# Self-attention scores of a perceiver layer: by key alone, with the row of maxima spread through HBM and the values one token tile later

## The chip, the core and the metric

The kernel runs on one core of a Trainium2 chip, as one launch. The metric is the device time of that launch in microseconds (us), as the median of several runs. The engines of the core have their own instruction queues: TensorE (PE; its weight loads are shown apart as PEld), VectorE (DVE), ScalarE (ACT), GpSimd (POOL) and SyncE (SP), which issues most DMAs here. TensorE writes to PSUM, which this kernel uses as eight banks of 128 x 512 fp32; ScalarE and VectorE bring results from there to SBUF.

## The reference, cut to what matters

The input is x of 16 batches x 64 tokens x 1024, and a context of 16 x 1024 x 1024. Three blocks follow each other, each added to x:

```python
x = x + xattn(layernorm(x), ctx, ctx)    # 32 heads, 8 key/value heads, head size 32, 1024 keys a batch
x = x + attn(layernorm(x))               # the same heads, biases, rotary, 64 keys a batch
x = x + ffn(layernorm(x))                # ternary weights, 4-bit and 8-bit activations, 1024 -> 2752 -> 1024
```

The change is in the second block. What it computes there, per batch and head (four query heads share a key/value head):

```python
scores = einsum('bqhd,bkhd->bhqk', q, k) / sqrt(32)
probs  = softmax(scores, axis=-1)        # over the 64 keys of the batch
out    = einsum('bhqk,bkhd->bqhd', probs, v)
```

The softmax takes a maximum over the keys for each query and head, subtracts it, and divides by the sum of the exponentials.

## The kernel before

The 1024 tokens are 8 tiles of 128 tokens, so a tile holds two whole batches. The order of the work on every engine is the order in which the program names it: there is no planner. Side work for TensorE waits in a list, `fillers`, and each `fill(n)` in the program takes the next n of them. The loop over the tiles (L1242 to L1289) is the place of the change.

SBUF is one large tile, `arena`, in which buffers are placed by hand (`place`, in KB), and rings hand out two or more places in turn. PSUM has two banks `m0`, `m1` that `m_tile` gives in turn, two more (`t0`, `t1`) for transposes, and four for `w`, the scores and outputs of the attention. There is only one `w`.

**A tile of self attention** (class `Tile2`) needs the scores twice, since the maximum over the keys lies along the free dimension only when queries are the partitions, and the values need the keys as partitions:

- `by_query`: 32 matmuls give scores with queries as partitions in `w` (L770, K = 32 rows, four row groups of the array side by side); one VectorE reduction takes the maxima over 64 keys (L778).
- `shift` (`in_parts`, L539 to L546): four small VectorE instructions split each maximum into three bfloat16 parts.
- `turn`: eight TensorE transposes (L787) bring the parts under each other, one ScalarE copy (L793) takes them to SBUF.
- `by_key`: eight matmuls against a matrix of minus ones (L802, shown as L801) write the negative maxima into `w`, 16 fp32 matmuls (L813) add the scores with keys as partitions; ScalarE takes the exponential straight from PSUM (L821).
- `values`: 16 matmuls for the outputs (L834) and 16 for the sums (L845), both into `w`, three ScalarE copies (L853, L856).
- `finish`: 12 transposes into `w` (L866, L869), VectorE's reciprocal and two products (L871, L876), and POOL adds the result to the residual `xs[t]` (L882).

An fp32 matmul is shown as two instructions.

**Beside it.** With a tile's result in `xs[t]`, `quantize(t)` makes the 4-bit activations in three pieces: statistics (L179 to L185, with a power on POOL), normalize and the mean magnitude (L171, L914), and rounding (L917 to L925); `transpose3` turns them for the feed-forward part (L932, copied by ScalarE, L933).

**The fillers.** In the early tiles 0 to 3 they are 24 steps of `project2(1)`, the projections for batches 8 to 15: four halves for the two key chunks, four steps for v and 16 halves for the eight query chunks, where a half is the matmuls of four of the eight slices of the sum (L242) and a v step is a whole chunk (L730). A q or k chunk is taken from its bank by ScalarE with the bias (L709); then the rotary follows on VectorE (L710, L711) and POOL (L712, L713). A v chunk is taken by VectorE (L737). In the late tiles 4 to 7 the fillers are 32 calls of `gate_up` for the first four token tiles: eight matmuls for the gate into one bank, eight for the up part into the other (L950), a relu on ScalarE (L958), a product on VectorE (L959) and one on POOL (L962). A relu and a product per filler set the two `m` banks free. Two of the 24 run ahead of the loop and 6, 6, 5 and 5 in tiles 0 to 3. Ahead of tile 4 two gate/up steps run, then up to eight in each tile.

Behind the loop comes the rest of the feed-forward part: quantize of tile 7, and gate/up steps for tiles 4 to 7.

**The first attention** (class `Unit`) already works by key alone: VectorE collects maxima, turns them by 32x32 block transposes and reductions (L591 to L598), SP writes the row to HBM and reads it back to all partitions (L604, L605), VectorE subtracts it (L610) and ScalarE takes the exponential (L611).

Of the kernel before, what the change touches and what calls it, by code (L numbers as in the profile page):

```python
# [20 lines left out]
P = 128  # L21
# [28 lines left out]
def kernel(  # L50
# [33 lines left out]
    def t_tile(shape, dtype, name, n=None):  # L84

        turns["t"] ^= 1
        n = turns["t"] if n is None else n
        return ps_t.tile(shape, dtype, tag=f"t{n}", name=name)
# [14 lines left out]
    def place(kb, shape, dtype=F32):  # L103

        first, n = round(kb * 256), math.prod(shape) * mybir.dt.size(dtype)
        a = arena[:, first : first + (n + 3) // 4]
        if dtype != F32:
            a = a.bitcast(dtype)
        a = a[:, : math.prod(shape)]
        if len(shape) > 1:  # L110
            names = [f"a{i}" for i in range(len(shape))]
            sizes = dict(zip(names[1:], shape[1:]))
            a = a.rearrange(f"p ({' '.join(names)}) -> p {' '.join(names)}", **sizes)
        return a
# [46 lines left out]

    spilled = [dram.tile([P, DIM], F32, name=f"spilled{t}") for t in range(NT)]
    results = [dram.tile([P, DIM], F32, name=f"results{t}") for t in range(NT - 2)]
    tops = [dram.tile([1, 1024], F32, name=f"tops{i}") for i in range(2)]

    def layernorm(dst, src, name):
# [372 lines left out]
    def in_parts(to, m):  # L539

        rest = small.tile([P, 32], F32, tag="rest")
        rest = rest[:, : math.prod(m.shape[1:])].rearrange("p (a b) -> p a b", b=m.shape[2])
        nc.vector.tensor_copy(to[:, :, :, 0], m)
        nc.vector.tensor_tensor(rest, m, to[:, :, :, 0], ALU.subtract)
        nc.vector.tensor_copy(to[:, :, :, 1], rest)
        nc.vector.tensor_tensor(to[:, :, :, 2], rest, to[:, :, :, 1], ALU.subtract)  # L546
# [129 lines left out]
    n2s = {}  # L676
    kT2 = place(112, [2, B, NQ])
    v2 = place(120, [NT, KVD])
    sh2_ring = Ring(152, 154)
    oS = place(156, [2, 4, 2, NQ])  # L680
    sS = place(160, [4, 2, NQ])
    parts2 = [place(162 + 2 * i, [8, 4, HD], BF) for i in range(2)]
    p2_ring = Ring(136, 144)
    biased_ring = Ring(172, 174)
    turned_ring = Ring(168, 170)
# [70 lines left out]
    class Tile2:  # L756
# [3 lines left out]
        def __init__(self, t, w):  # L760
            self.t, self.w = t, w

        def by_query(self):
            t = self.t
            s = self.w.rearrange("p j (c k) -> p j c k", k=NQ)
            for c in range(8):
                b2, g, rp = c // 4, c // 2 % 2, c % 2
                for jj in range(4):
                    rows = bass.ts(jj, HD)
                    nc.tensor.matmul(  # L770
                        s[:, jj, c, :],
                        lhsT=qa[g][rows, bass.ds((2 * t + b2) * 256 + rp * P, P)],
                        rhs=kT2[rows, g, 2 * t + b2, :],
                        start=True,
                        stop=True,
                    )
            top = small.tile([P, 4, 8], F32, tag="top32", name=f"top2_{t}")
            nc.vector.tensor_reduce(top, s, AX.X, ALU.max)  # L778
            self.top = top

        def shift(self):
            in_parts(parts2[self.t % 2], self.top.rearrange("p j c -> p c j"))

        def turn(self):
            tp = t_tile([P, 8 * P], BF, f"shp2_{self.t}")
            for c in range(8):
                nc.tensor.transpose(  # L787
                    tp[:, bass.ts(c, P)],
                    parts2[self.t % 2][:, c].rearrange("p j k -> p (j k)"),
                    ident_b,  # L790
                )
            self.sh = sh2_ring.next([2, 2, 256], BF)
            nc.scalar.copy(self.sh.rearrange("p b g c -> p (b g c)"), tp)  # L793

        def by_key(self):
            t = self.t
            s = self.w.rearrange("p j (g c) -> p j g c", g=2)
            for b2 in range(2):
                for jj in range(4):
                    rows = bass.ts(jj, HD)  # L800
                    nc.tensor.matmul(  # L801
                        self.w[bass.ts(b2, NQ), jj, :],  # L802
                        lhsT=minus[rows, 0:NQ],
                        rhs=self.sh[rows, b2].rearrange("p g c -> p (g c)"),
                        start=True,
                        stop=False,
                    )
            for g in range(2):
                for b2 in range(2):
                    for jj in range(4):  # L810
                        rows = bass.ts(jj, HD)
                        b = 2 * t + b2
                        nc.tensor.matmul(  # L813
                            s[bass.ts(b2, NQ), jj, g, :],
                            lhsT=kT2[rows, g, b, :],
                            rhs=qa[g][rows, bass.ts(b, 256)],
                            start=False,
                            stop=(g == 1),
                        )
            self.p = p2_ring.next([4, 2, 256])  # L820
            nc.scalar.activation(  # L821
                self.p.rearrange("p j g c -> p (j g c)"),
                self.w.rearrange("p j c -> p (j c)"),
                AF.Exp,
                scale=SCALE,
            )

        def values(self):
            t, p, w = self.t, self.p, self.w
# [75 lines left out]
    def quantize(t):  # L905

        xn = place(xn3_at, [DIM])
        statistics, normalize = layernorm(xn, xs[t], f"n3_{t}")
        b = beta[:, t : t + 1]
        rb = small.tile([P, 1], F32, tag="rb", name=f"rb_{t}")  # L910

        def magnitude():
            normalize()
            nc.vector.tensor_reduce(b, xn, AX.X, ALU.add, apply_absolute_value=True)  # L914

        def rounded():
            nc.vector.tensor_scalar_mul(b, b, 1.0 / DIM)  # L917
            nc.vector.tensor_scalar_add(rb, b, EPS)
            nc.vector.reciprocal(rb, rb)
            nc.vector.tensor_scalar(xn, xn, SQRT7, rb, ALU.mult, ALU.mult)  # L920
            nc.vector.tensor_scalar(xn, xn, -8.0, 7.0, ALU.max, ALU.min)
            xq3[t] = place(xq_at, [DIM], BF)
            nc.vector.tensor_scalar(xq3[t], xn, MAGIC, MAGIC, ALU.add, ALU.subtract)
            nc.gpsimd.tensor_tensor(cgate[:, t : t + 1], b, wscale[:, 0:1], ALU.mult)
            nc.gpsimd.tensor_tensor(cup[:, t : t + 1], b, wscale[:, 1:2], ALU.mult)  # L925

        return [statistics, magnitude, rounded]
# [113 lines left out]
    def fill(n=1):  # L1041
        for _ in range(n):
            if fillers:
                fillers.pop(0)()

    with tc.manual_schedule():
# [174 lines left out]
        nc.sync.dma_start(bv_sb, bv.to_broadcast([P, KVD]))  # L1221
        for g in range(2):
            wqs2.append(load_queries(stream.next([4, KC, P]), wq2[g], nc.sync, 1))
        for p in parts2:
            nc.gpsimd.memset(p, 0.0)


        for n, step in enumerate(project2(0)):
# [10 lines left out]
        ps_w2 = ps_w_closed.enter_context(tc.tile_pool(name="ps_w2", bufs=1, space=PSUM))  # L1239
        w = ps_w2.tile([P, 4, 512], F32, name="w2")  # L1240
        fill(2)
        for t in range(NT):  # L1242
            two = Tile2(t, w)
            late = t >= NT // 2
            if t == NT // 2 - 2:
                for n in range(2):
                    fetch(n)
            if t == NT // 2:
                fill(len(fillers))
                fetch(2)  # L1250
                steps = [(n, tt) for n in range(NCH) for tt in range(NT // 2)]

                steps[:12] = [s for s in steps[:12] if s[1] < 3] + [(n, 3) for n in range(3)]

                def beside(n, tt):
                    gate_up(n, tt, lambda i: m_tile(f"gu_{n}_{tt}_{i}"))
                    if tt == NT // 2 - 1:
                        fetch(n + 3)

                fillers += [lambda s=s: beside(*s) for s in steps]  # L1260
                fill(2)
            pieces = quantize(t - 1) if t else []

            def piece():
                if pieces:
                    pieces.pop(0)()

            two.by_query()
            fill()
            two.shift()  # L1270
            fill()
            two.turn()
            fill()
            piece()
            if late:
                fill()
            piece()
            two.by_key()
            fill()
            piece()  # L1280
            if late:
                fill()
            two.values()
            fill()
            two.finish()
            if t:
                transpose3(t - 1)
            if t % 4 < 2 or late:
                fill()  # L1289
        fill(len(fillers))  # L1290

# [107 lines left out]
```

## Time and profile before

| | |
|---|---|
| median of 3 runs | 1881.87 us (1881.67 to 1883.24) |
| the profiled execution | 1883.46 us, span 1881.5 us |
| granted TensorE clock, mean | 0.997 |
| first and last scores by query of the self attention (L770) begin | 1488.6 and 1685.4 us |
| mean of one block transpose of 128x1024 (L591) | 1245 ns |
| mean of one subtraction of 128x2048 (L610) | 2957 ns |
| spread of a row to 128 partitions, 512 KB (L605), median landing | 4.4 us |

The page gives busy time and share of each engine, and groups of instructions by line. TensorE's weight loads overlap its matmuls, and a busy TensorE is not one at its peak. The timeline gives start and duration of instructions in order; in brackets stands how long the engine was idle before one, and what released it. The windows give the same busy times for chosen stretches, with the granted clock.

### The profile page before, as it was taken

To read this page: it belongs to the slowest core of one execution; us is meant where nothing else is said; L and a number is where in the kernel's file an instruction comes from. 1 tells how busy PE (TensorE), PEld (TensorE's weight loads), DVE (VectorE), ACT (ScalarE), POOL (GpSimd) and SP (SyncE) were. 2 spreads that over 40 slices of the span, in tenths; PEclk is the share of its full clock that TensorE was granted. 3 is DMA by queue.
4 is the path that set the end of the run, shared out by engine and by line. 5 is a ranking of instruction groups with operands and counts; after the bars stand their busy time and mean duration, and the time that the engine had idled before them with its cause. 6 is when DMAs were issued, how large, how long until landed. Compare 5 with 4: busy or idle time off the path is not lost.

```text
span 1881.5 us, 27514 instructions
## 1 busy us (share of the span) xinstructions
PE 1844.0 (98%) x11520; PEld 1099.2 (58%) x11520; DVE 1200.9 (64%) x1396; ACT 891.8 (47%) x916; POOL 876.5 (47%) x481
## 2 busy tenths in 40 slices
PE   8999999999899999999999999999999999999999
PEld 5445556565565665665665665664445554665654
DVE  3011587777777887887887887877523245665564
ACT  1233656656566766766766766543100112333221
POOL 1000447655575674674674674663413433444420
PEclk9999999999999999999999999999999999999999
DMA  9234468777687877877877877744020000113201
GB/s 343 69 105 144 181 220 274 221 231 247 176 252 214 251 239 213 257 233 217 257 229 219 260 226 206 202 156 175 5 90 0 1 31 16 47 53 101 71 29 51
DMA packets 63499, 306.19 MB, mean 163 GB/s; under 512 B 8784, under 2 KB 17936, under 8 KB 47632
## 3 DMA queue, kind: packets, MB, share of 16 engines
q1 hardware_dynamic: 54160, 243.63, 36.6%
q0 software_dynamic: 8064, 58.72, 15.5%
q10 hardware_dynamic: 1152, 2.10, 0.3%
q8 instruction: 90, 1.47, 0.3%
q14 instruction: 33, 0.27, 0.0%
HBM read 285.35 MB, written 19.07 MB: 162 GB/s over the span
## 4 chain that ended last, share of the span: by engine, by line
PE 69%; DMA 1%; POOL 1%; ACT 1%; DVE 1%; issue 0%; POOLq 0%; DVEq 0%; ACTq 0%
PE v L418 15%; PE z L399 10%; PE wo L242 6%; PE q L242 6%; PE t L567 5%; PE o L629 5%; PE d L1024 4%; PE g L950 4%; PE gu L950 4%; PE p L399 3%; PE v L730 1%; PE k L242 1%; DMA arena<-in_ctxT 1%; POOL arena L620 1%; PE w L770 1%; PE o L639 1%
## 5 line engine op out<-in xcount | busy, mean ns | idle before, releaser
L620 POOL TENSOR_TENSOR arena<-arena 128x1024 f32<-128x1024 f32 x192 | 541.6, 2821 | 20.5 <-ACT arena L611 8.5
L418 PE MATMUL v<-arena 128*128 128x256 f32 x1792 | 405.2, 382 | 1.2 <-ACT arena L434 1.2
L586 DVE TENSOR_TENSOR arena<-t,arena 128x512 f32<-128x512 f32 x384 | 258.7, 687 | 212.8 <-PE t L567 156.0
L418 PEld LDWEIGHTS v<-arena 128*128 128x128 f32 x1792 | 336.8, 190 | 78.3 <-issue 29.3
L610 DVE TENSOR_TENSOR arena<-arena 128x2048 f32<-128x2048 f32 x128 | 373.5, 2957 | 4.7 <-DMA arena<-tops 4.7
L579 ACT COPY arena<-t 128x1024 f32<-128x1024 f32 x256 | 254.9, 1009 | 208.5 <-PE t L567 119.1
L611 ACT ACTIVATE arena<-arena 128x2048 f32<-128x2048 f32 x128 | 244.6, 1911 | 168.5 <-DVE arena L610 167.6
L617 POOL TENSOR_TENSOR arena<-arena 128x1024 f32<-128x1024 f32 x32 | 76.4, 2388 | 526.9 <-ACT arena L611 502.6
L399 PE MATMUL z<-arena 128*128 128x512 f32 x560 | 260.3, 607 | 12.1 <-DMA arena<-in_ctxT 7.9
L242 PE MATMUL q<-arena 128*128 128x512 f32 x512 | 225.4, 596 | 0.6 <-ACT arena L279 0.6
L399 PEld LDWEIGHTS z<-arena 128*128 128x128 f32 x560 | 103.2, 192 | 138.9 <-issue 118.9
L242 PEld LDWEIGHTS q<-arena 128*128 128x128 f32 x512 | 95.3, 190 | 115.9 <-issue 113.7
L567 PE MATMUL t<-arena 32*128 32x256 f32 x2048 | 146.6, 400 | 1.2 <-ACT arena L338 1.2
L583 DVE TENSOR_REDUCE arena<-t 128x512 f32<-128x1024 f32 x64 | 74.7, 1204 | 91.8 <-PE t L567 91.8
L567 PEld LDWEIGHTS t<-arena 32*128 32x128 f32 x2048 | 93.1, 184 | 66.6 <-issue 61.4
L950 PEld LDWEIGHTS <-arena 128*128 128x128 bf16 x1024 | 98.1, 97 | 57.5 <-issue 6.6
L629 PE MATMUL o<-arena 128*32 128x256 f32 x2048 | 123.8, 382 | 0.0
L962 POOL TENSOR_TENSOR arena<-arena 128x344 f32<-128x344 f32 x64 | 70.8, 1108 | 107.7 <-DVE arena L959 96.9
L242 PE MATMUL wo<-arena 128*128 128x512 f32 x256 | 112.3, 595 | 0.3 <-ACT arena L279 0.3
L399 PE MATMUL p<-arena 128*128 128x512 f32 x224 | 108.2, 605 | 0.0
L629 PEld LDWEIGHTS o<-arena 128*32 128x32 f32 x2048 | 60.0, 109 | 68.7 <-issue 32.0
L712 POOL TENSOR_TENSOR arena<-arena 128x512 f32<-128x512 f32 x20 | 35.5, 1773 | 123.1 <-DVE arena L710 123.1
(149 smaller groups left out, 1960.2 us busy)
## 6 DMA issues: line engine op xcount, KB each, us to landing
arena<-in_ctxT SPq DMA_DIRECT2D x31, 2048.0 KB, 12.0
arena<-in_ctxT POOLq DMA_DIRECT2D x56, 1024.0 KB, 11.1
arena<-in_ctxT SPq DMA_DIRECT2D x28, 1024.0 KB, 10.0
arena<-in_wg SPq DMA_DIRECT2D x32, 688.0 KB, 4.5
arena<-in_wu SPq DMA_DIRECT2D x32, 688.0 KB, 5.8
arena<-in_wd SPq DMA_DIRECT2D x32, 688.0 KB, 8.8
arena<-tops SPq DMA_DIRECT2D x32, 512.0 KB, 4.4
arena<-ternary SPq DMA_DIRECT2D x32, 344.0 KB, 3.5
```

The costliest lines, as they stand in the source:

```text
L242: nc.tensor.matmul(made[0], lhsT=lhsT(k), rhs=rhs(k), start=(k == 0), stop=(k == KC - 1))
L399: nc.tensor.matmul(held[n], lhsT=weights[:, k, :], rhs=what()[:, k, :], start=(first and k == 0), stop=(k == 3), skip_group_check=not first,)
L418: nc.tensor.matmul(held[n][:, bass.ts(at, KVD)], lhsT=ctx_halves[b, h][:, k, bass.ts(kts[at], P)], rhs=wkvs[:, k, KVD:], start=(k == 0), s ...
L567: nc.tensor.matmul(ws[jj // 2][:, jj % 2, a, :], lhsT=self.kT[rows, self.g, bass.ts(i * 2 + a, P)], rhs=two_tiles[self.b // 2 % 2][rows, s ...
L579: nc.scalar.copy(pt[:, 2 * mine : 2 * mine + 2], ws[mine])
L586: nc.vector.tensor_tensor(m, w[:, :, a], m, ALU.max)
L610: nc.vector.tensor_tensor(pt, pt, by.to_broadcast([P, 4, 2, 256]), ALU.subtract)
L611: nc.scalar.activation(pt, pt, AF.Exp)
L617: nc.gpsimd.tensor_tensor(acc, pt[:, :, 0], pt[:, :, 1], ALU.add)
L620: nc.gpsimd.tensor_tensor(acc, acc, pt[:, :, a], ALU.add)
L629: nc.tensor.matmul(self.po[bass.ts(jj, HD), 0:256], lhsT=self.v[:, kt, bass.ts(self.g * 4 + jj, HD)], rhs=self.pts[i][:, jj, a, :], start= ...
L950: nc.tensor.matmul(ps[:, :CW], lhsT=xqT[t][:, k, :], rhs=wbs[n][i][:, k, :], start=(k == 0), stop=(k == KC - 1),)
```

## The change

The scores are computed once, with the keys as partitions. `by_query`, `shift` and `turn` go, and so do the minus products in `by_key`. In their place:

- `by_key` now ends with two ScalarE copies of `w` into `self.p`, a VectorE block transpose and a reduction for each half, eight 32x32 transposes and a last reduction that give one row of 2048 maxima for each of the two batches. SP writes the rows to HBM (`tops2`, 16 KB) and reads each back to the 64 partitions of its batch (`shift2`, 512 KB each).
- `exponentials`, new, subtracts `shift2` on VectorE and takes the exponential on ScalarE, both in place in `self.p`.
- The loop makes nine passes. Pass t starts with the exponentials of tile t-1, then the scores of tile t, then `transpose3` of tile t-2, then the values and `finish` of tile t-1, and the pieces of quantize of tile t-1. The places of the fillers move with it: 4, 7, 7 and 4 of the 24 steps in passes 0 to 3, and eight gate/up steps in each of the passes 4 to 7. Pass 8 has none left.
- Buffers move: `shift2` and `blocks2` share the 8 KB at 158, `oS` and `sS` lie 4 KB lower, the places of the parts and of the turned shift go.

```diff
+    tops2 = [dram.tile([2, 2048], F32, name=f"tops2_{i}") for i in range(2)]
...
-    sh2_ring = Ring(152, 154)
-    oS = place(156, [2, 4, 2, NQ])
-    sS = place(160, [4, 2, NQ])
-    parts2 = [place(162 + 2 * i, [8, 4, HD], BF) for i in range(2)]
+    oS = place(152, [2, 4, 2, NQ])
+    sS = place(156, [4, 2, NQ])
+
+    shift2, blocks2 = place(158, [2048]), place(158, [2048])
+    quarters2 = place(198, [4, 2, HD])
+    turned2 = place(199, [4, HD])
...
-        def by_query(self):
...
-        def shift(self):
...
-        def turn(self):
...
         def by_key(self):
             t = self.t
             s = self.w.rearrange("p j (g c) -> p j g c", g=2)
-            for b2 in range(2):
-                for jj in range(4):
-                    rows = bass.ts(jj, HD)
-                    nc.tensor.matmul(
-                        self.w[bass.ts(b2, NQ), jj, :],
-                        lhsT=minus[rows, 0:NQ],
-                        rhs=self.sh[rows, b2].rearrange("p g c -> p (g c)"),
-                        start=True,
-                        stop=False,
-                    )
...
-                            start=False,
-                            stop=(g == 1),
+                            start=True,
+                            stop=True,
                         )
             self.p = p2_ring.next([4, 2, 256])
-            nc.scalar.activation(
-                self.p.rearrange("p j g c -> p (j g c)"),
-                self.w.rearrange("p j c -> p (j c)"),
-                AF.Exp,
-                scale=SCALE,
+            flat = self.p.rearrange("p j g c -> p (j g c)")
+            top = small.tile([P, 2 * HD], F32, tag="top2", name=f"top2_{t}")
+            for i in range(2):
+                cols = bass.ts(i, 1024)
+                nc.scalar.copy(
+                    flat[:, cols], self.w[:, 2 * i : 2 * i + 2].rearrange("p j c -> p (j c)")
+                )
+                nc.vector.transpose(blocks2[:, cols], flat[:, cols])
+                nc.vector.tensor_reduce(
+                    top[:, bass.ts(i, HD)],
+                    blocks2[:, cols].rearrange("p (b k) -> p b k", k=HD),
+                    AX.X,
+                    ALU.max,
+                )
+
+
+            for q in range(4):
+                for i in range(2):
+                    nc.vector.transpose(
+                        quarters2[0:HD, q // 2 * 2 + i, q % 2, :],
+                        top[bass.ts(q, HD), bass.ts(i, HD)],
+                    )
+            nc.vector.tensor_reduce(
+                turned2[0:HD], quarters2[0:HD].rearrange("p n q c -> p n c q"), AX.X, ALU.max
             )
+            rows = tops2[t % 2]
+            nc.sync.dma_start(
+                rows.rearrange("b (i p c) -> p (b i) c", i=2, c=HD), turned2[0:HD]
+            )
+            for b2 in range(2):
+                nc.sync.dma_start(
+                    shift2[bass.ts(b2, NQ)], rows[b2 : b2 + 1].to_broadcast([NQ, 2048])
+                )
+
+        def exponentials(self):
+            flat = self.p.rearrange("p j g c -> p (j g c)")
+            nc.vector.tensor_tensor(flat, flat, shift2, ALU.subtract)
+            nc.scalar.activation(flat, flat, AF.Exp, scale=SCALE)
...
-        for p in parts2:
-            nc.gpsimd.memset(p, 0.0)
...
-        for t in range(NT):
-            two = Tile2(t, w)
+        two, last = None, None
+        for t in range(NT + 1):
+            two, last = (Tile2(t, w) if t < NT else None), two
             late = t >= NT // 2
...
                 fillers += [lambda s=s: beside(*s) for s in steps]
-                fill(2)
-            pieces = quantize(t - 1) if t else []
-
-            def piece():
-                if pieces:
-                    pieces.pop(0)()
-
-            two.by_query()
+            if last:
+                last.exponentials()
+            if two:
+                two.by_key()
             fill()
-            two.shift()
+            if t > 1:
+                transpose3(t - 2)
             fill()
-            two.turn()
-            fill()
-            piece()
-            if late:
+            pieces = []
+            if last:
+                last.values()
                 fill()
-            piece()
-            two.by_key()
-            fill()
-            piece()
-            if late:
+                last.finish()
+                pieces = quantize(t - 1) if t < NT else []
+            else:
                 fill()
-            two.values()
-            fill()
-            two.finish()
-            if t:
-                transpose3(t - 1)
-            if t % 4 < 2 or late:
+            fill(2 if late else 1)
+            for piece in pieces:
+                piece()
                 fill()
         fill(len(fillers))
```

More of the change, by code (lines that the diff above doesn't have):

```diff
@@ L761, in __init__ @@
             self.t, self.w = t, w
-        def by_query(self):
[L764 to L767, printed above, removed]
-                for jj in range(4):
-                    rows = bass.ts(jj, HD)
[L770 to L773, printed above, removed]
-                        start=True,
-                        stop=True,
-                    )
-            top = small.tile([P, 4, 8], F32, tag="top32", name=f"top2_{t}")
-            nc.vector.tensor_reduce(top, s, AX.X, ALU.max)
-            self.top = top
-        def shift(self):
-            in_parts(parts2[self.t % 2], self.top.rearrange("p j c -> p c j"))
-        def turn(self):
[L785 to L793, printed above, removed]
         def by_key(self):
@@ L797, in by_key @@
             s = self.w.rearrange("p j (g c) -> p j g c", g=2)
-            for b2 in range(2):
-                for jj in range(4):
-                    rows = bass.ts(jj, HD)
-                    nc.tensor.matmul(
-                        self.w[bass.ts(b2, NQ), jj, :],
-                        lhsT=minus[rows, 0:NQ],
-                        rhs=self.sh[rows, b2].rearrange("p g c -> p (g c)"),
-                        start=True,
-                        stop=False,
-                    )
             for g in range(2):
```

## The prediction

> **What bounds the kernel now.** I read first the page's span and busy shares, then TensorE's timeline through one late tile of the self attention, then the places where TensorE waits there.
>
> ```profile
> span 1881.5 us, 27514 instructions
> PE 1844.0 (98%) x11520; PEld 1099.2 (58%) x11520; DVE 1200.9 (64%) x1396; ACT 891.8 (47%) x916; POOL 876.5 (47%) x481
> ```
>
> TensorE is busy for 98% of the span. What it no longer does is saved only where it finds its next operands and banks ready.
>
> ```profile
> 1658.63 2.01 PE L770 MATMUL w<-arena 32*128 32x64 f32 x64
> 1660.57 4.87 PE L950 MATMUL gu<-arena 128*128 128x344 fp8e4 x32
> 1665.49 0.62 PE L787 MATMUL shp<-ident_b,arena 128*128 128x128 bf16 x8
> 1665.95 4.86 PE L950 MATMUL gu<-arena 128*128 128x344 fp8e4 x32
> 1670.74 0.42 PE L801 MATMUL w<-arena,minus 32*64 32x512 bf16 x8
> 1670.98 1.04 PE L813 MATMUL w<-arena 32*64 32x256 f32 x32
> 1671.96 5.07 PE L950 MATMUL gu<-arena 128*128 128x344 fp8e4 x32
> 1676.96 1.09 PE L834 MATMUL w<-arena 64*32 64x256 f32 x32
> ...
> 1681.22 0.60 PE L866 MATMUL w<-ident,arena 128*128 128x128 f32 x4
> ```
>
> One late tile (start, duration, instructions): no holes, the next begins at 1685.41, so 26.8 us. Eight gate/up fillers of 2.43 us (half of 4.87) lie between the attention's pieces. Each uses two banks, gate then up, and the next filler uses the same two: its gate matmuls wait for ScalarE's relu of the filler before, its up matmuls for VectorE's product (L959).
>
> ```profile
> 1713.26 1.29 DVE L179 BATCH_NORM_STATS2 st_n<-arena 128x6 f32<-128x512 f32 x2 [2.51 <-POOL arena L882]
> ...
> 1714.90 0.58 DVE L959 SCALAR_TENSOR_TENSOR arena<-gu,cup,arena 128x344 f32<-128x344 f32 x1
> ...
> 1715.53 2.45 PE L950 MATMUL gu<-arena 128*128 128x344 fp8e4 x8 [2.60 <-DVE arena L959]
> ```
>
> Just behind the loop this goes wrong once: VectorE has statistics ahead of the product in its order, and TensorE stands 2.60 us for the bank. It also comes back slow: these 8 matmuls take 2.45 us, against 1.22 elsewhere, and the granted clock is halved:
>
> ```profile
> 1713.00:1715.00 2.00, 0.00 (x0) 0.00 (x0) 1.67 (x5) 0.55 (x1) 0.23 (x1) 0.98 1.01 323
> 1715.00:1717.00 2.00, 1.47 (x6) 0.79 (x6) 1.84 (x2) 0.00 (x0) 1.89 (x3) 0.50 0.11 33
> 1717.00:1719.00 2.00, 2.00 (x11) 1.13 (x10) 1.73 (x3) 0.00 (x0) 1.00 (x2) 0.66 0.00 1
> ```
>
> Columns: stretch, length, busy PE, PEld, DVE, ACT, POOL, granted clock, DMA. Half clock from 1715.5 to about 1718.4 costs some 1.6 us.
>
> **What the change removes from TensorE.** Per tile, from start to next start: scores by query 1.94 (1658.63 to 1660.57), the shift's transposes 0.46, the minus products 0.24: 2.64 us, 21.1 us for 8 tiles. ScalarE loses the copy of the turned shift (1.01) and keeps an exponential (1.88 from PSUM, 1.91 from SBUF by L611). VectorE loses the maximum (2.29) and four small ones (1.0). The two memsets of L1225 go (POOL, 1.9 us): nothing waited for them.
>
> **What it adds.** ScalarE: two copies of 128x1024, 1.01 each (L579). VectorE: the first attention does the same things.
>
> ```profile
> 1302.96 1.25 DVE L591 STREAM_TRANSPOSE arena<-arena 128x1024 f32<-128x1024 f32 x1
> 1304.24 1.22 DVE L593 TENSOR_REDUCE top<-arena 128x32 f32<-128x1024 f32 x1
> 1305.49 0.84 DVE L597 STREAM_TRANSPOSE arena<-top 32x32 f32<-32x32 f32 x4
> 1306.37 0.36 DVE L598 TENSOR_REDUCE arena<-arena 32x32 f32<-32x128 f32 x1
> ```
>
> Two transposes and two reductions with their gaps are 5.05 us, eight small transposes 1.68. The last reduction reads 256 elements: between 0.36 (128) and 1.22 (1024), interpolated 0.49. The subtraction of 128x2048 is L610: lowest 2.28, mean 2.96, highest 5.14; POOL is light in late tiles, so I take 2.6. [...]
>
> DMA on SP: a write of 16 KB and two broadcasts of 512 KB per tile. The rows nearest are L604 (4 KB, 1.3 us to landing, 4.0 at most) and L605 (512 KB, 4.4); the farthest, 2 MB of wkv in 14.5. I take 1.5 + 0.7 issue + 6 = 8.2 us, between 5 and 19. Weight fetches queue behind them on SP, but are asked for three chunks (about 29 us) ahead: nothing.
>
> **The new order of a late tile.** VectorE and ScalarE work in program order. Ahead of the first filler's relu and product now stand subtraction, exponential, both copies and the whole chain of maxima. Count from s, when VectorE is free for the subtraction of tile t-1: subtraction to 2.6, exponential to 4.6, copies to 5.7 and 6.7, relu of filler 1 to 7.3; transposes and reductions 5.7 to 10.8, small ones to 12.5, last reduction 13.0, product of filler 1 13.6. TensorE meanwhile has the scores (1.04), filler 1 (2.43) and the transposes of xq (0.45), then stands for the relu, does the second gate (1.2), and stands until 13.7 for the second up. After that up 1.2, values 1.9, filler 3 2.4, the 12 transposes of finish with their wait for the copies 1.5, and 1.6 for the halved clock: finish ends at 22.3. Behind it (call that F) VectorE is last again: fillers 4 and 5 end at F+4.9, product 5 at F+5.6, statistics (1.75, after POOL's residual sum at F+4.3) 7.35, POOL's power 8.05, normalize and sum 10.15, product 7 10.75, rounding 3.1, product 8 F+14.75. There s begins anew: 22.3 + 14.75 = 37.05 us a tile, with some 11 us of idle TensorE.
>
> **The early tiles.** Count from the first tile (1488.60). Their fillers are halves of a projection (3.5 us), mostly evicted by ScalarE, so VectorE's lag matters less. Tile 0 with four fillers ends at 15.5; its chain of maxima ends at 9.6, the spread lands at about 18. Tile 1: subtraction 18 to 21, chain done at 31.5; TensorE stands for the copies (2 us), then for the bank of a v chunk that VectorE empties only behind the chain (27.3 to 32): ends at 51. Tile 2 is dense with seven fillers: ends at 81.4. Tile 3 has the last four, waits some 4 us for the copies, and is done at 105; the last rotary on POOL ends at 110, and VectorE, with quantize of tile 2 uncovered, is free at 116 (111 to 119 by the subtraction's and the DMA's bounds). Before, the first gate/up stood at 1598.99, 110.4: TensorE gets there as early, VectorE is late.
>
> **The drain.** An added ninth pass has no filler left (all 32 are used in tiles 4 to 7): subtraction, exponential 4.7, values at half clock 3.6, copies 1.75, finish 1.4: 11.5 us with hardly any cover; the spread itself has long landed.
>
> **The sum.** After, finish of tile 7 ends at 116 + 4 x 37.05 + 11.5 = 275.7; before at 1708.80, 220.2. What follows is alike in both (statistics of tile 7, held by POOL, start 4 us behind). So +55.5 us on the profiled execution's 1883.46 (span 1881.5 and 1.96 around it): 1939.0. That execution lies 1.6 above the median 1881.87, so 1937 as a median. The removed 21.1 us are inside it. Bounds: with subtraction 2.28, no loss of clock and VectorE free at 111, 111 + 4 x 35.1 + 9.6 = 261, +41, 1923; with 5.1 for the subtraction and 119, 119 + 4 x 39.6 + 14 = 291, +71, 1953.
>
> On the clock: the rows show half speed after 2.60 us of standing. [...] No run here yet shows waits of 5 us.
>
> **Rivals.** (1) *VectorE runs ahead.* If quantize's tail were done early, each late tile would begin with VectorE some 5 us further: period near 32.4, 245 in all, +25: 1907. For it: VectorE is busy only 16 of 27 us before. Against: subtraction follows the last product in its order, and that needs TensorE's last up matmul. (2) *Not slower.* The fillers hide the chain: -21.1, and 4.8 for the drain (6.5 idle less the 1.7 that finish waits now): 1866. It decides at the second up matmuls: product 1 must be done within about 4 us of the scores' end (filler 1, transposes, second gate); I have over 11. (3) *The spread comes late.* It has 37 - 13 = 24 us before it is wanted; beyond that every us costs about 7. At 28 us it is 1965. For it: a wait on tops already stands at L610 (4.7, once); against: no landing in the trace above 18.1, and DMA is at 0.01 to 0.39 here.
>
> **Chances.** My sum 0.72, (1) 0.13, (2) 0.07, (3) 0.08. The bounds and most of (1) make the range 1905 to 1958; it leaves out (2), (3) and the lower edge of (1). One measurement tells 0.2% (3.8 us) from no change. Faster 0.06 and the same 0.01, both from (2); slower 0.93.
>
> **What would show it.** The rows of by_query and the minus products are gone; TensorE waits on gu for VectorE (about 5 us, each late tile) and for ScalarE's relu (about 5); scores of tiles 5, 6, 7 start 37 us apart; the granted clock of the late tiles falls below 0.95; the subtraction waits for DMA in tile 1 alone; some 7 us of hole before the last values. I am wrong if late tiles are under 31 us apart, or if VectorE waits for the spread in most tiles.

## The result and the profile after

The changed kernel takes 1924.45 us (median of four runs, 1923.59 to 1925.94) against 1882.38 us beside it: a ratio of 1.0224, 95% interval 1.0206 to 1.0242. It is slower, by 42 us. The forecast was 1937 us in a range of 1905 to 1958: sign and range hold, and the time is 12.6 us lower than said.

The page of the changed kernel, its span, engines and the TensorE clock in 40 slices:

```profile
span 1924.2 us, 26359 instructions
...
PE 1842.2 (96%) x10880; PEld 1087.1 (56%) x10880; DVE 1237.9 (64%) x1468; ACT 897.8 (47%) x924; POOL 883.8 (46%) x479
...
PEclk9999999999999999999999999999999997888999
```

TensorE has 640 matmuls fewer, yet is busy for about as long as before (1844.0), and the clock sags in four slices, which hold the late tiles and the drain. The windows say how that fits together. Each line is the stretch from the first scores to the end of the last `finish`, the first of before, the second of after (start and end, length, busy PE, PEld, DVE, ACT, POOL with their instructions, granted clock, DMA share, GB/s):

```profile
1488.60:1708.80 220.20, 213.57 (x2273) 133.22 (x2273) 122.52 (x211) 65.04 (x88) 87.06 (x80) 1.00 0.14 40
```

```profile
1487.93:1750.79 262.86, 211.42 (x1642) 121.17 (x1641) 160.25 (x283) 72.17 (x97) 96.38 (x80) 0.87 0.26 67
```

The stretch grew by 42.7 us, as much as the span (1881.5 to 1924.2), so all of the loss is here. TensorE's idle time grew from 6.6 to 51.4 us: 44.8. Its busy time fell by only 2.2 although 21.1 us of work went: for the other 19 us the work that stayed takes longer, nearly all of it at a lower clock, which counts as busy (the gate/up matmuls alone have 89.4 us in place of 79.0 for as many instructions). 44.8 - 2.2 is the 42.7, but for rounding.

What TensorE waited for in that stretch (line waiting, line that released it; us in total, times, longest):

```profile
PE gu L943 <- ACT arena L951: 14.8, 3, 5.8
PE gu L943 <- DVE arena L952: 11.9, 4, 3.2
PE gu L943 <- ACT arena L926: 5.4, 1, 5.4
PE w L774 <- POOL arena L716: 4.2, 1, 4.2
PE w L827 <- ACT arena L819: 4.0, 1, 4.0
PE q L243 <- DVE arena L740: 4.0, 1, 4.0
PE w L827 <- ACT arena L786: 3.8, 3, 2.7
...
```

In the numbering of the kernel after, L943 are the gate/up matmuls, L951 their relu, L952 the product, L774 the scores by key, L827 the values, L786 the copies of the scores, L819 the exponential and L926 the copy of the turned xq. The two costliest lines are gate/up fillers that stand for a bank. The third is one filler of pass 5 that reads the xq turned just before it: it waits for that copy, which stands behind the relu on ScalarE. TensorE's timeline of one late tile, which answers the dense one of before:

```profile
1669.32 1.12 PE L774 MATMUL w<-arena 32*64 32x256 f32 x32
1670.37 2.52 PE L943 MATMUL gu<-arena 128*128 128x344 fp8e4 x16
1672.73 0.61 PE L925 MATMUL xqp<-ident_b,arena 128*128 128x128 bf16 x8
1677.81 2.45 PE L943 MATMUL gu<-arena 128*128 128x344 fp8e4 x8 [4.47 <-ACT arena L951]
1683.46 2.45 PE L943 MATMUL gu<-arena 128*128 128x344 fp8e4 x8 [3.21 <-DVE arena L952]
1685.85 1.45 PE L827 MATMUL w<-arena 64*32 64x256 f32 x32
...
1690.89 1.04 PE L862 MATMUL w<-ident,arena 128*128 128x128 f32 x8
1691.76 11.91 PE L943 MATMUL gu<-arena 128*128 128x344 fp8e4 x80
1703.60 1.12 PE L774 MATMUL w<-arena 32*64 32x256 f32 x32
```

Scores to scores: 34.28 us against 26.8. The gate of filler 2 stands 4.47 us for the relu of filler 1, its up part 3.21 us for the product of filler 1, and eight matmuls take 2.45 us in place of 1.22. Why relu and product are late is on the other two timelines, ScalarE's and VectorE's of the same tile:

```profile
1673.58 1.91 ACT L819 ACTIVATE arena<-arena 128x2048 f32<-128x2048 f32 x1 [4.72 <-DVE arena L818]
1675.39 1.91 ACT L786 COPY arena<-w 128x1024 f32<-128x1024 f32 x2
1677.19 0.56 ACT L951 ACTIVATE arena<-gu,cgate 128x344 f32<-128x344 f32 x1
```

```profile
1670.78 0.57 DVE L952 SCALAR_TENSOR_TENSOR arena<-gu,cup,arena 128x344 f32<-128x344 f32 x1
1671.26 2.28 DVE L818 TENSOR_TENSOR arena<-arena 128x2048 f32<-128x2048 f32 x1
1676.42 1.25 DVE L789 STREAM_TRANSPOSE arena<-arena 128x1024 f32<-128x1024 f32 x1 [2.88 <-ACT arena L786]
...
1681.25 1.24 DVE L800 STREAM_TRANSPOSE arena<-top 32x32 f32<-32x32 f32 x8
1682.52 0.41 DVE L804 TENSOR_REDUCE arena<-arena 32x128 f32<-32x256 f32 x1
1682.86 0.55 DVE L952 SCALAR_TENSOR_TENSOR arena<-gu,cup,arena 128x344 f32<-128x344 f32 x1
```

ScalarE sat idle for 4.72 us ahead of the exponential, which waits for VectorE's subtraction (L818); the copies of scores that were ready at 1670.4 and the relu stand behind it. VectorE in turn waits 2.88 us for the copies, and the product of filler 1 stands behind the whole chain of maxima, until 1682.86. Neither engine is full; both are held by their order. From the first subtraction of the late passes to the last VectorE is busy for 83.57 of 137.66 us and ScalarE for 41.50 (columns as above, the granted clock is 0.84):

```profile
1602.09:1739.75 137.66, 103.92 (x934) 64.45 (x935) 83.57 (x149) 41.50 (x60) 50.73 (x47) 0.84 0.28 71
```

### The profile page after: what moved, and what is told of

Its sections match the earlier page's. It is cut to its first block, busy times and chain, and to the rows that moved or that the text cites. A ratio compares the mean times of both kernels' runs of the same rounds, so it can differ in the third digit from the quotient of the medians.

```text
span 1924.2 us, 26359 instructions
## 1 busy us (share of the span) xinstructions
PE 1842.2 (96%) x10880; PEld 1087.1 (56%) x10880; DVE 1237.9 (64%) x1468; ACT 897.8 (47%) x924; POOL 883.8 (46%) x479
## 5 line engine op out<-in xcount | busy, mean ns | idle before, releaser
L400 PE MATMUL z<-arena 128*128 128x512 f32 x560 | 261.7, 610 | 11.5 <-ACT arena L580 4.9
L943 PEld LDWEIGHTS <-arena 128*128 128x128 bf16 x1024 | 102.1, 101 | 96.3 <-issue 35.2
L955 POOL TENSOR_TENSOR arena<-arena 128x344 f32<-128x344 f32 x64 | 78.8, 1232 | 137.2 <-DVE arena L952 130.9
L943 PE MATMUL gu<-arena 128*128 128x344 fp8e4 x544 | 94.5, 334 | 35.1 <-DVE arena L952 14.9
```

The lines of the kernel that those rows point to most:

```text
L400: nc.tensor.matmul(held[n], lhsT=weights[:, k, :], rhs=what()[:, k, :], start=(first and k == 0), stop=(k == 3), skip_group_check=not first,)
L943: nc.tensor.matmul(ps[:, :CW], lhsT=xqT[t][:, k, :], rhs=wbs[n][i][:, k, :], start=(k == 0), stop=(k == KC - 1),)
L955: nc.gpsimd.tensor_tensor(inter[t][:, bass.ts(c, CW)], prod, relu, ALU.mult)
```

## The experiments

The theory: relu and product of the first filler stand in program order behind the subtraction, the exponential, the copies and the chain of maxima; the next filler needs the same two banks; so TensorE idles, and then runs at half clock. Rivals: the spread through HBM is late; VectorE has too much work, whatever its order; ScalarE's order alone does it. All the diffs are cut to their core.

**Without the chain of maxima and the spread.**

```diff
-                nc.vector.transpose(blocks2[:, cols], flat[:, cols])
-                nc.vector.tensor_reduce(top[:, bass.ts(i, HD)], ...)
...  (the small transposes, the last reduction and the three DMAs go too)
-            nc.vector.tensor_tensor(flat, flat, shift2, ALU.subtract)
+            nc.vector.tensor_tensor(flat, flat, <ones, broadcast>, ALU.subtract)
```

> The changed kernel without the chain of maxima and without the spread: no block transposes, no reductions, no writes to or reads from HBM; the subtraction takes away the constant 1 from every score instead of the maxima of the keys (softmax is the same for any constant per query, so only the guard against large scores is left out). Order of all else unchanged. Theory (products of the fillers stand behind VectorE's chain, relus behind ScalarE's exponential and copies): the wait for the product goes, the wait for the relu (4.5 us a late tile) stays. The second up matmuls start some 3.4 us earlier in each late tile and lose less clock: late tiles 30 to 31 us apart instead of 34.3; early passes win about 5. Expected 1904 us, 1898 to 1910. Rival (it is VectorE's added load as such that costs): near or below the kernel before, 1882 or less. Rival (it is the order subtraction, exponential, copies on ScalarE alone): no more than 3 us gained, 1921 or more.

Measured: 1898.26 us, ratio 1.0085 (1.0070 to 1.0100). TensorE's late tile:

```profile
1652.63 0.61 PE L903 MATMUL xqp<-ident_b,arena 128*128 128x128 bf16 x8
1657.71 4.05 PE L921 MATMUL gu<-arena 128*128 128x344 fp8e4 x16 [4.47 <-ACT arena L929]
1661.69 1.15 PE L805 MATMUL w<-arena 64*32 64x256 f32 x32
```

The wait for the product is gone and the wait for the relu is the same 4.47 us. Tiles are 29.92 us apart. So the chain and the spread together are worth 26 of the 42 us, and 16 us of loss remain with neither: a late spread can't be the cause of those, and VectorE's load as such isn't either, since it is busy for 25.3 of 50 us here (1630 to 1680 us), where it was for 30.4 before the change (1650 to 1700 us). Whether the 26 us are the chain's length or its place, this run doesn't tell; chain_between below does.

**Copies ahead of the exponential.**

```diff
+            if last:
+                last.exponentials()      # between the two copies of the new scores and their transposes
...
-            if last:
-                last.exponentials()      # ahead of by_key
```

> Same work as the changed kernel, one reordering: in each pass the two copies of the new scores stand ahead of the exponentials of the tile before on ScalarE, so that the chain of maxima follows the subtraction on VectorE at once. Theory: the chain starts 2.9 us earlier (the hole VectorE has today between subtraction and first transpose), the relu comes 1.8 us earlier; late tiles 31.4 us apart instead of 34.3, early passes win about 5 with the shorter waits for the copies. Expected 1907 us, 1902 to 1913. Rival (the length of VectorE's and ScalarE's work ahead of the evictions does not matter, the halved clock or the ninth pass do): 1920 or more.

Measured: 1905.14 us, ratio 1.0124 (1.0107 to 1.0141). TensorE's late tile:

```profile
1658.35 2.40 PE L947 MATMUL gu<-arena 128*128 128x344 fp8e4 x8 [2.64 <-ACT arena L955]
1663.07 2.45 PE L947 MATMUL gu<-arena 128*128 128x344 fp8e4 x8 [2.31 <-DVE arena L956]
```

In the late tiles VectorE's chain follows its subtraction within 0.1 us, and the wait for the relu falls to 2.64 us in the last two. The waits for the product stay, at 1.3 to 3.4 us. This tile lasts 32.7 us, not the 31.4 that were expected: values and sums, behind the second wait, run longer at half clock (the values 1.96 us, where they have 1.09 at full speed; 3.44 us from their start to the next filler, where the tile shown of the changed kernel has 2.24). ScalarE's order is part of the loss (some 19 us), not all of it. More than half of that lies in the early tiles, where the wait for the copies goes altogether: from the first scores to the first gate/up matmul 99.4 us pass in place of 110.0.

**A third bank for the fillers.**

```diff
-                    gate_up(n, tt, lambda i: m_tile(f"gu_{n}_{tt}_{i}"))
+                    gate_up(n, tt, lambda i: third(f"gu_{n}_{tt}_{i}"))   # m0, m1, t0 in turn; transpose3 in t1
```

> Same work and order as the changed kernel, but the gate/up fillers in the loop rotate over three PSUM banks (one of the two banks for transposes joins, transpose3 keeps the other). Theory: TensorE stands because both banks wait for their evictions. With a third bank the second gate runs at once, the second up waits for the relu (about 3.3 us), the values run, and only the third gate waits for the first product, some 1.3 us. Finish comes about 4.5 us earlier in each late tile: 29.8 us apart instead of 34.3, expected 1906 us, 1900 to 1912. The early passes do not change. Rival (TensorE is held by VectorE's total work per tile, not by banks): 1921 or more.

Measured: 1910.65 us, ratio 1.0151 (1.0136 to 1.0166): the direction holds, the gain is 4 to 5 us short. TensorE's late tile:

```profile
1664.78 1.34 PE L951 MATMUL gu<-arena 128*128 128x344 fp8e4 x8
1669.40 1.33 PE L951 MATMUL gu<-arena 128*128 128x344 fp8e4 x8 [3.29 <-ACT arena L959]
...
1675.07 3.98 PE L951 MATMUL gu<-arena 128*128 128x344 fp8e4 x16 [2.44 <-DVE arena L960]
```

The gate of filler 2 now runs at once, and its up part and filler 3 stand instead, 3.29 and 2.44 us. One bank more moves the waits back by one group of matmuls; the evictions are as late as they were (the product of filler 1 starts 11.6 us behind the subtraction in both kernels). Tiles are 31.12 us apart, where 29.8 was expected: filler 3 waits 2.44 us, not 1.3, and comes back at half clock. In pass 5 a wait of 1.99 us for a weight fetch is new.

**Useless matmuls in the holes.** This puts a price on the clock: TensorE waits as before, but doesn't stand.

```diff
+            if NT > t > 4:
+                idle_work(t, 0, 16)                     # ahead of filler 2: 16 matmuls, result unused
+                beside2(lambda: idle_work(t, 1, 14))    # between its gate and up parts: 14
```

> The changed kernel with useless matmuls in the two holes of passes 5, 6 and 7: 16 bfloat16 products of 128x128 by 128x512 (about 0.21 us each) ahead of the second gate, 14 ahead of the second up, into a bank that nothing reads. Theory: they end before the waits end, so that they cost nothing, keep the granted clock at 1.0, and the second up and the values run at full speed: 1.2 to 1.6 us less in each of the three passes, 1920 us in all (1918.5 to 1921.5), the second up 1.2 instead of 2.4 us. Rival (the halved clock lies off the path): 1924.5, unchanged within 1. If they overrun their holes: above 1926.

Measured: 1922.21 us (1916.34 to 1923.81), ratio 1.0208 (1.0187 to 1.0229). That lies outside the 1918.5 to 1921.5 that were expected, and the medians can't tell it from the 1.0224 of the change. The useless matmuls take 0.23 us each (3.62 us for 16), where about 0.21 was said. The trace shows where the gain is and where it goes:

```profile
1672.58 3.62 PE L939 MATMUL idle<-arena,ident_b 128*128 128x512 bf16 x16
1677.20 1.33 PE L956 MATMUL gu<-arena 128*128 128x344 fp8e4 x8 [1.01 <-ACT arena L964]
1678.38 3.18 PE L939 MATMUL idle<-arena,ident_b 128*128 128x512 bf16 x14
1682.87 1.33 PE L956 MATMUL gu<-arena 128*128 128x344 fp8e4 x8 [1.31 <-DVE arena L965]
1684.13 1.09 PE L827 MATMUL w<-arena 64*32 64x256 f32 x32
```

The up part starts as late as it did (14.15 us behind the scores' start, 14.14 after the change), so the order sets it; but it takes 1.33 in place of 2.45 us and the values 1.09 in place of 1.45, and tiles are 32.81 us apart, not 34.28: half clock costs 1.5 us a tile on the path. The slower gate matmuls cost nothing, since what follows them waits anyway. In the profiled execution the three passes win 4.5 us together, and the drain behind them loses 1.25 again (12.63 us from the last transposes of xq to the next gate/up matmuls, where it was 11.38): there the half clock now lasts into the transposes of `finish`, 1.91 us in place of 1.04.

**The chain laid between the fillers.** The same instructions in another order: scores, copies, then the subtraction, filler 1, the exponential, half of the chain, filler 2, values, the other half and the spread, filler 3, `finish`, the rest. Two gate/up steps run ahead of pass 4, and five of those that belong behind the loop are moved into pass 8. In the early tiles the chain stays whole, and the fillers are 6, 6, 5 and 5.

```diff
-            if last:
-                last.exponentials()
             if two:
                 two.by_key()                 # scores and copies
-            fill()
+            if last:
+                last.subtract()
...  (early passes: both halves of the chain, the spread and the exponential here)
+            fill(counts[0])
+            if last and late:
+                last.exponentials()
             if t > 1:
                 transpose3(t - 2)
-            fill()
+            if two and late:
+                two.maxima(0)
+            fill(counts[1])
             if last:
                 last.values()
+            if two and late:
+                two.maxima(1)
+                two.spread()
...  (the counts of the fillers, and the five steps moved into pass 8)
```

> All work of the changed kernel, other order: the copies of the new scores stand first on ScalarE; in the late passes the subtraction stands ahead of filler 1, the exponential behind its relu, the first half of the maxima ahead of filler 2, the second half and the spread ahead of filler 3, behind the values. So no product of a filler has more than about 2.5 us of VectorE in front of it, except where the values run beside. Early fillers are 6, 6, 5, 5 and two gate/up steps run ahead of pass 4, as in the kernel before; five gate/up steps of the last four tiles run in pass 8, beside subtraction, exponential and copies. Theory (order ahead of the evictions is the cause): the waits for gu nearly vanish, late passes 24 to 26 us apart (work of TensorE in one: 24.1), the removed 21 us of TensorE come out as gain: 1868 us (1860 to 1880), faster than the kernel before. Rival (VectorE's and ScalarE's added work cannot be hidden): above 1895.

Measured: 1877.39 us, ratio 0.9974 (0.9962 to 0.9987), faster than the kernel before the change by a quarter of a percent. The late tile of pass 6:

```profile
1652.21 1.12 PE L774 MATMUL w<-arena 32*64 32x256 f32 x32
1653.27 2.52 PE L951 MATMUL gu<-arena 128*128 128x344 fp8e4 x16
1655.63 0.61 PE L933 MATMUL xqp<-ident_b,arena 128*128 128x128 bf16 x8
1656.07 2.51 PE L951 MATMUL gu<-arena 128*128 128x344 fp8e4 x16
1658.51 1.09 PE L835 MATMUL w<-arena 64*32 64x256 f32 x32
...
1675.91 1.12 PE L774 MATMUL w<-arena 32*64 32x256 f32 x32
```

23.70 us, with no hole, and 3.1 us less than the 26.8 of before the change: here the 2.64 us of removed matmuls are gained. Maxima, spread, subtraction and exponential are all still there, so the loss was one of order. It isn't gone everywhere: in passes 2 to 5 TensorE still waits some 18 us, 5.0 of them for a product and 4.4 for the turned xq, and 1877 lies 9 us above the 1868 that was expected, though inside its range.

**The same with a third bank, and with a bare end.**

```diff
-        EXTRA = 5
+        EXTRA = 0                            # between_bare_end: the five gate/up steps behind the loop again
...
-            (2, 1, 1, 1),
+            (0, 0, 0, 0),                    # no filler in pass 8
```

> As chain_between, and the gate/up fillers of the loop rotate over three banks. Theory: what is left of the waits for product and relu goes too; 2 to 4 us less than chain_between, 1866 us (1858 to 1878). If chain_between has no waits left: the same within 1 us.

> As chain_between, but pass 8 has no fillers, as in the changed kernel: subtraction, exponential and the copies of the last tile lie bare. Theory: 5 to 8 us more than chain_between (in the changed kernel the three holes of pass 8 are 1.5, 4.0 and 1.7 us, and the values behind them run at half clock).

Measured: with the third bank 1872.25 us, ratio 0.9951 (0.9936 to 0.9966). With a bare pass 8 1888.04 us, ratio 1.0028 (1.0017 to 1.0039): 10.7 us above chain_between, more than the 5 to 8 expected. (The third bank is worth 5.1 us, where 2 to 4 was expected.) The bare end brings back the waits of the changed kernel:

```profile
1706.94 1.96 PE L835 MATMUL w<-arena 64*32 64x256 f32 x32 [4.00 <-ACT arena L827]
1708.65 1.96 PE L846 MATMUL w<-arena,pick 64*32 64x256 f32 x32
1712.33 0.66 PE L867 MATMUL w<-ident,arena 128*128 128x128 f32 x4 [1.72 <-ACT arena L857]
```

and, behind the loop, a wait of 3.05 us for a product, as the changed kernel has at the same place. The last of the three waits shown, and one of 2.60 us behind the loop, stood in the kernel before the change too, so not all of the 10.7 us are new with the ninth pass. The bare end by itself takes back more than twice what chain_between gains. It also parts the 47 us between the changed kernel and chain_between: 10.7 are the end, and 36 remain for the order of everything else, in which the chain's place and the places of the early fillers were not told apart.

**Two moves of the fillers.** `transpose3` behind filler 2, with one step fewer in pass 4 and one more in pass 8, and one early step moved from pass 1 to pass 3 (later_turns); then more fillers ahead of the values in passes 1, 2, 3, 5 and 8, two steps fewer in pass 4, and the exponential of the early passes behind their first fillers too (fillers_ahead).

```diff
-            if t > 1:
-                transpose3(t - 2)
             fill(counts[1])
+            if t > 1:
+                transpose3(t - 2)
             if last:
                 last.values()
```

```diff
-            (1, 1, 1, 1, 1, 0, 0),           # fillers of pass 1 at its seven places
+            (2, 2, 1, 0, 0, 0, 0),
...  (so in passes 2, 3 and 5; three steps in place of five in pass 4; seven steps in pass 8, five ahead of its values)
```

> As between_three_banks, and transpose3 stands behind filler 2, ahead of the values, so that rounding of the tile before has one filler more time and the values cover ScalarE's copy; the first gate/up step of token tile 3 comes one filler later, and pass 4 takes one step less. Theory: what is left in between_three_banks are TensorE's waits for rounding (6.3 us in four places), for the copy behind it (4.4 us in pass 5) and for pass 4's late VectorE (about 5), and some half clock behind them; the first two go, 8 to 12 us less: 1863 us (1858 to 1868). Rival (the waits move to another place, since VectorE is busy for some 22 of 24 us in a late pass): 1870 or more.

> The kernel of later_turns with the same fillers moved within their passes: every pass, the early ones too, has its first fillers ahead of the values, the exponential always stands behind the first of them, and pass 8 keeps seven gate/up steps, five of them ahead of its values. Theory (in later_turns TensorE still stands 9.6 us in four places ahead of values for an exponential that is late because VectorE ends its rounding late in passes 2, 3 and 5, and its matmuls come back at half clock behind three of these): with more work ahead of the values those waits shrink, 6 to 10 us less than later_turns' 1870.8, so 1863 (1859 to 1869). Rival (VectorE itself is behind there, so that any place for the fillers only moves the waits to another line, as from between_three_banks to later_turns): 1869 to 1874, with the waits of the values smaller and others, for a bank or for the rounding, as much larger.

Measured: later_turns 1870.79 us, ratio 0.9940 (0.9926 to 0.9953), 1.5 us better than between_three_banks where 8 to 12 were hoped for, and the two intervals overlap: here the rival was right, that the waits move to another place (1870 or more). fillers_ahead 1882.71 us, ratio 0.9998 (0.9989 to 1.0006), 12 us worse. Where TensorE waits in later_turns, and then in fillers_ahead:

```profile
PE w L843 <- ACT arena L835: 9.6, 4, 3.5
PE gu L959 <- DMA arena<-ternary: 2.1, 1, 2.1
...
```

```profile
PE gu L959 <- DVE arena L968: 11.2, 3, 6.5
PE w L782 <- DVE arena L885: 8.8, 3, 5.2
PE gu L959 <- DMA arena<-ternary: 3.2, 1, 3.2
...
```

The values' wait for the exponential goes, as the theory of fillers_ahead had it, but what was taken from behind `finish` is missing there: the next scores (L782) need `w`, which VectorE empties with the products of `finish` (L885), and they stand up to 5.2 us. Two fillers in a row at the head of a pass wait 6.5 us for a product. The rival, that the waits only move, has the direction right, and its 1869 to 1874 is too low. The best of these kernels, later_turns, is 12.0 us faster than before the change.

## Why the prediction was right, and where its sum was off

**The mechanism** was the stated one. `by_query` and the minus products are gone from the rows; TensorE waits in each late tile for the product of the first filler, and in all but one for its relu; in pass 5 it is the copy of the turned xq behind that relu (5.37 us), which the prediction didn't name. Every unfilled wait named for the early tiles is there: for the copies (0.63 and 2.73 us where 2 and 4 were said, and 0.40 in tile 2, which was said to be dense), for the bank of a v chunk (4.00, where 4.7 was said), and for the last rotary on POOL (the second half of the scores starts at 108.9 us behind the first, said: rotary done at 110).

**The sum.** Counted from the first scores:

| term | predicted | measured |
|---|---|---|
| VectorE free for pass 4 | 116 | 114.2 (1602.09) |
| a late tile, by the starts of the subtraction | 37.05 | 34.3, 34.2 (the last two); mean of four 34.4 |
| four of them | 148.2 | 137.7 |
| drain: subtraction in pass 8 to the end of `finish` | 11.5 | 11.0 (1739.75 to 1750.79) |
| end of the last `finish` | 275.7 | 262.9 |

The step that failed in size is the late tile: 10.5 of the 12.8 us. By its own parts, with s at 1671.26: the second up part at s+12.2, not 13.7, of which 0.3 is the subtraction (2.28 taken, where I put 2.6) and 0.9 the chain of maxima (1676.42 to 1682.86, 6.4 us where I had 7.3: the eight small transposes take 1.24 in place of 1.68, the last reduction 0.41 in place of 0.49); from there to the end of `finish` 8.3, not 8.6; and from that end to the next s 13.8, not 14.75, of which 0.3 stands in none of its parts (10.75, rounding 3.1 and a product of 0.6 are 14.45). Each was a little high, none offset another, and the sum goes round four times. The subtraction has a median of 2282 ns (2275 to 3356) over eight in this trace. The longest ran beside POOL's products of the rotary (L715, L716); in four of the late passes it kept its 2.28 us, and the filler's product that POOL began beside it (L955) took 2.89 us, where most others have 0.91.

**The clock.** 1.6 us a late tile was taken, and idle_matmuls shows 1.5. The clock below 0.95 is in the windows: 0.84 over the late passes.

**The drain.** Said 11.5, measured 11.0. Covering it, and the wait behind it, is worth 10.7 us in between_bare_end.

**The early tiles** were right to a microsecond: tiles 0, 1 and 2 end at 15.0, 51.0 and 80.7 us, where 15.5, 51 and 81.4 were said. For tile 1 this is luck: its waits are 2.1 us shorter than said, and the eight matmuls behind the wait of 4.00 us take 6.0 us to the next start in place of 3.5, at a clock of 0.58, which the sum didn't have.

**Rival 1**, VectorE ahead, fell: in each of the last three passes the subtraction starts right behind a product, as the rows above show for one. **Rival 2**, not slower, fell for this order, at the point named for it: product 1 is done 13 us behind the scores' end, and 4 was the limit. That it isn't beyond reach shows in chain_between, where the late tile has no hole. **Rival 3**, the late spread, fell: VectorE waited once for the row, in pass 1, as said:

```profile
DVE arena L818 <- DMA arena<-tops: 2.2, 1, 2.2
```

The write lands in 1.4 us, the two broadcasts in 6.2 (median), about the 8.2 in all that were taken.

**Smaller misses.** The waits per late tile are 4.47 and 3.21 us where "about 5" was said for both. The second is shorter above all because the gate matmuls ahead of it take 2.45 us at half clock, where 1.2 was said, inside the time that the product takes anyway. VectorE's four small instructions that went have 1.65 us in the late tile before, not 1.0; no term of the sum rests on them. What stays open is how much of the removed 21.1 us can be had at all: the best kernel here has 12.0, and still some 16 us of waits from the first scores to 1790 us, in places that move with the fillers.

## What to carry to other kernels

When work moves from a busy engine to idle ones, look first at what stands behind it in their program order: a PSUM eviction of half a microsecond behind a chain of 11 us idles TensorE for most of that chain (7.7 us in a late tile here), though VectorE and ScalarE are far from full. Lay such a chain in pieces between the evictions, and put what waits for another engine (here the exponential) behind what is ready (the copies). A pipeline made one stage deeper has a drain, and work must be kept for it: here covering the end was worth 10.7 us.

## What was not expected of the hardware

Whether a hole halves the clock isn't a matter of its length alone. In third_bank eight matmuls behind a hole of 3.29 us took the full-speed 1.33 us, and 16 behind the next hole of 2.44 us took 3.98 in place of about 2.5. One pass later, behind the same two holes of 3.29 and 2.44 us, both ran at full speed (1.34 and 2.51). In later_turns a hole of 2.11 us, for a weight fetch, slowed what followed: 48 matmuls took 8.88 us, where 80 have 11.91 at full speed, and the granted clock is 0.50 at 1637 to 1639 us. The granted clock of third_bank is 1.00 in the 4 us behind the first hole and 0.50 at 1676 to 1678 us, behind the second.

What decides it beside the length, no run here measured; the cause is open.

Eight 32x32 block transposes in a row took 1.24 us, 155 ns each; four in a row in the first attention had 0.84, 210 ns each.
